# Layer 2's q by seven products, with PSUM rings kept by hand, in a four-layer attention network on one core

## The chip, the core and the metric

The kernel runs on one core of a Trainium2 chip. All data are f32. The metric is the device time in microseconds (us) of one execution. The program is given as a median of several executions; a profile comes from one further execution, which has its own time and, inside it, a span from the first to the last record.

## What is computed

The reference takes x of 4 images with C = 512 channels and 32x32 = 1024 tokens, and sends it through four residual layers, each on a normalised input (groups of 16 channels in layers 0 to 3, `_gn`):

```python
# layer 0: attention with mixed heads, 8 heads of 64
q, k, v = w_q @ x, w_k @ x, w_v @ x
attn = softmax(w_head . (q^T k * hd**-0.5))           # heads mixed ahead of the softmax
attn = instance_norm(attn) * gamma + beta             # over each head's 1024x1024
x = x + (attn @ v) @ w_proj.T + b_proj
# layer 1: a gate for each channel from the channel means, through a 9-qubit circuit
x = x + gn(x) * sigmoid(circuit(mean(gn(x))) @ fc_w.T + fc_b)
# layer 2: plain attention, 8 heads
q, k, v = Wq @ gn(x) + bq, Wk @ gn(x) + bk, Wv @ gn(x) + bv
x = x + Wp @ (softmax(q^T k / 8) applied to v) + bp
# layer 3: each token attends to its 8 best of 2048 memory rows
x = x + softmax(top8(x_t @ mem.T)) @ mem
```

## The kernel before

**Stages.** `first()` loads image 0 and normalises it block by block (128 channels a block, KC = 4) while q is multiplied. The layer-0 stage then goes through the images one after another: for each, 32 steps of 32 query rows (`step`), a software pipeline in which the scores of step s, the head mixing of step s-2 and the product with v of step s-7 stand together. After the 32 steps, seven more (`STEPS` to `STEPS + LAG`) empty the pipeline; there the next image's q products are made, a block a step. Then come its k products. The output projection of an image is spread over the steps of the next; the last image's follows at the end of the stage (`put_out`). Layer 1 is a scaling that is folded into the coefficients with which layer 2's input is normalised.

**Layer 2** is a loop over the images, with 16 units each: a unit is the scores of four key blocks against 512 queries of two heads (`scores2`), their exp on ScalarE, and the product with v of the unit before (`apply2`). `pair_sum` and `sums2` gather the sums of exp on GpSimd and VectorE, `over_keys` turns them, `invert2` sums them over the partitions on TensorE, inverts them and sends them through DRAM to be broadcast (`rb`), and `finish2` multiplies the output in PSUM by them. The end of one image and the beginning of the next is called a border here: the next image's q, k and v are multiplied, and then the output projection of this one (`seven_out`), with the first scores of the next ahead of it. Layer 3 follows.

**Seven products.** At the borders k, v and the output projection are made by `seven` (L1031): a 512x512 by 512x1024 product is cut into 2x2 quarters and made of seven products of quarters, four 128x512 matmuls of two records each, thus 28 in place of 32. They need sums of quarters of the input (`input_sums`: five VectorE operations, 128x1024 each) and of the weights (`weight_sums`: five of 128x512), and sums of the products, added from PSUM by VectorE. The weights' sums overwrite two quarters of the weights in place and fill three further places (`places7`); they are made once, for image 1, and stored to DRAM for the later images (`w_sums`). q is made of eight quarter products, by `project` (L192) through `take_q2` (L1140), and evacuated by VectorE, which adds the bias and scales it by 1/8.

**PSUM.** There are eight banks of 128x512. In the layer-0 stage they are three pairs (`pairs`), `pv_bank` and `pt_bank`, chosen by index. At the change to layer 2 the pool is closed, and two new pools are opened, of three pairs (`ps_s`) and two banks (`ps_m`); these hand out buffers in the order of allocation. Small products (`small_ps`: group means and row sums) take a pair there.

**Order.** Much of the order is written out by hand: `pin` keeps instructions in program order on their engine, which holds for the products, the copies out of PSUM and most VectorE operations. What isn't pinned is placed by a scheduler. DMAs are issued by SyncE (SP), ScalarE and GpSimd, each a queue of its own.

**Lines that the steps touch.** L312/L313 statistics, L145 group means and L326 normalising in the start; L332 q of image 0; L292 ScalarE's copy of q (`put_q`); L532 product with v of layer 0, and L590 to L592 `take_out`, the copy of the finished tile out of `pv_bank`; L684 the output's last addition at the stage's end; L1183 scores of layer 2; L1177 its exp; L1056 products by channels in `seven`; L1073 ScalarE's bias copy in `seven_k`; L1220 the product with v of layer 2; L1251 the row sums.

In the tail of layer 0, `step` has `piece` (the q product and its copy L292) between the last product with v and `take_out`:

```python
        if not tiled or s >= STEPS:
            piece(b, s)
        if mixing:
            ...
        if tiled and part == 3:
            take_out(b, j)
```

Of the kernel before, what the change touches and what calls it, by code (L numbers as in the profile page):

```python
# [16 lines left out]
P = 128  # L17
B = 4
C = 512
# [22 lines left out]
def fast_net(ctx: ExitStack, tc: tile.TileContext, a: dict, out: bass.AP, flag: bass.AP):  # L42
# [21 lines left out]
    def chan(src, name):  # L64
        t = const.tile([P, KC], F32, tag=name, name=name)
        nc.scalar.dma_start(out=t, in_=src)
        return t

    gamma = const.tile([P, NH], F32, tag="gamma", name="gamma")
    nc.scalar.dma_start(out=gamma, in_=a["in_gamma"].partition_broadcast(P))  # L70
    beta = const.tile([P, NH], F32, tag="beta", name="beta")
    nc.scalar.dma_start(out=beta, in_=a["in_beta"].partition_broadcast(P))
    bproj = chan(a["b_proj"], "bproj")
    bq2 = chan(a["bq"], "bq2")
    bk2 = chan(a["bk"], "bk2")
    bp2 = chan(a["bp"], "bp2")
    fcb = chan(a["fc_b"], "fcb")

    fcw = const.tile([NQ, C], F32, tag="fcw", name="fcw")
    nc.scalar.dma_start(out=fcw, in_=a["fc_w"])  # L80
    qpar = const.tile([P, NL * NQ], F32, tag="qpar", name="qpar")
    nc.scalar.dma_start(out=qpar, in_=a["q_params"].partition_broadcast(P))
# [3 lines left out]
    ident = const.tile([P, P], F32, tag="ident", name="ident")  # L86
    make_identity(nc, ident)
    ones = const.tile([P, P], F32, tag="ones", name="ones")
    nc.gpsimd.memset(ones, 1.0)
# [13 lines left out]
    )  # L103
    NS = 32
# [71 lines left out]
    def place(at, name):  # L176

        return pairs[at % 3] if at is not None else ps_s.tile([P, 2, NB], F32, tag="sc", name=name)
# [115 lines left out]
    def first():  # L294
# [3 lines left out]
        w = I["w_q"] = eight_k([P, KC, C], "w_q0_0", 0)  # L298
        for k in range(KC):
            nc.sync.dma_start(out=xn[:, k, :], in_=x_v[0, :, k, :])  # L300
            nc.sync.dma_start(out=w[:, k, :], in_=a["w_q"][:, k, :])
        I["w_k"] = load_w("w_k", "w_k0_0", 1)
# [5 lines left out]
        def stats(k):  # L308
            mv = small.tile([P, 2], F32, tag="mv0", name=f"mv0_{k}")
            st = small.tile([P, 2, 6], F32, tag="bnst", name=f"st_a0_{k}")  # L310
            for i in range(2):
                pin(nc.vector.bn_stats(st[:, i, :], xn[:, k, i * NB:(i + 1) * NB]))  # L312
# [3 lines left out]
        def means(k):  # L316
            next(parts[k])
            next(parts[k])
# [25 lines left out]
        for k in range(KC):  # L344
            if k + 2 < KC:
                stats(k + 2)
# [2086 lines left out]
```

## Time and profile before

| what | value |
| --- | --- |
| median of 3 executions | 2555.19 us (2554.56 to 2558.83) |
| profiled execution | 2558.39 us |
| its span | 2556.6 us |
| TensorE (PE) busy | 2503.3 us |
| VectorE (DVE) busy | 1685.8 us |
| ScalarE (ACT) busy | 985.8 us |
| GpSimd (POOL) busy | 1192.5 us |
| bytes moved | 361.39 MB, mean 141 GB/s |
| mean granted clock of TensorE | 0.998 |

The profile names groups of instructions by line, engine and operation: `pair<-xn_all,w_q` is a product into the PSUM pair from these two operands, and xN counts records. A f32 matmul of 128x128 by 128x512 is two records. "Waits" are idle times of an engine, with the engine that ended them and the line of the instruction on which it waited. The chain of waits is followed back from the last instruction of the program. Windows give busy times in a stretch of the span; PEclk is the share of full clock that TensorE was granted there.

### The profile page before, as it was taken

To read this page: it belongs to the slowest core of one execution; us is meant where nothing else is said; L and a number is where in the kernel's file an instruction comes from. 1 tells how busy PE (TensorE), PEld (TensorE's weight loads), DVE (VectorE), ACT (ScalarE), POOL (GpSimd) and SP (SyncE) were. 2 spreads that over 40 slices of the span, in tenths; PEclk is the share of its full clock that TensorE was granted. 3 is DMA by queue.
4 is the path that set the end of the run, shared out by engine and by line. 5 is a ranking of instruction groups with operands and counts; after the bars stand their busy time and mean duration, and the time that the engine had idled before them with its cause. 6 is when DMAs were issued, how large, how long until landed. Compare 5 with 4: busy or idle time off the path is not lost.

```text
span 2556.6 us, 47828 instructions
## 1 busy us (share of the span) xinstructions
PE 2503.3 (98%) x18534; PEld 1180.8 (46%) x18534; DVE 1685.8 (66%) x2785; ACT 985.8 (39%) x1177; POOL 1192.5 (47%) x1700
## 2 busy tenths in 40 slices
PE   8999999999999999999999999999999999999998
PEld 3344534554355534555633533453353344444445
DVE  4599448872688438881267567576657648788875
ACT  1467336651666336651153145125314612121211
POOL 3266415553465425553074147117405617566655
PEclk9999999999999999999999999999999999999999
DMA  2578438872698428982301130121014046767665
GB/s 83 145 207 237 125 120 226 244 211 74 172 243 235 131 82 211 244 248 101 124 16 55 70 112 18 54 83 59 21 54 148 18 130 190 219 186 217 187 184 170
DMA packets 187211, 361.39 MB, mean 141 GB/s; under 512 B 32729, under 2 KB 96217, under 8 KB 182882
## 3 DMA queue, kind: packets, MB, share of 16 engines
q1 hardware_dynamic: 105744, 178.71, 22.6%
q0 software_dynamic: 49152, 142.79, 20.6%
q10 hardware_dynamic: 32082, 36.76, 5.3%
q8 instruction: 149, 2.44, 0.4%
q14 instruction: 84, 0.69, 0.1%
HBM read 186.96 MB, written 36.96 MB: 88 GB/s over the span
## 4 chain that ended last, share of the span: by engine, by line
PE 74%; issue 10%; POOL 7%; DVE 3%; ACT 3%; DMA 2%; POOLq 0%; SPq 0%; ACTq 0%; DVEq 0%
PE pair L192 10%; PE sc_c L1183 9%; PE pv_c L1220 9%; PE pv L532 8%; POOL got L1360 7%; PE pair L467 6%; PE pair L493 5%; PE pt L425 5%; PE pt L721 4%; PE q L192 3%; PE Wk L1056 3%; PE Wv L1063 3%; ACT e L500 2%; PE Wp L1056 2%; PE at L1335 2%
## 5 line engine op out<-in xcount | busy, mean ns | idle before, releaser
L482 POOL DMA_DIRECT2D s<-ss x512 | 258.2, 511 | 399.5 <-PE pair L493 113.4
L506 DVE STREAM_TRANSPOSE eT<-e 128x1024 f32<-128x1024 f32 x256 | 316.5, 1236 | 193.6 <-ACT e L500 193.0
L1360 POOL DMA_INDIRECT got<-in_mem,ix x256 | 279.5, 1092 | 213.2 <-issue 122.1
L1177 ACT ACTIVATE eT<-sc_c 128x1024 f32<-128x1024 f32 x256 | 248.0, 1022 | 330.7 <-PE sc_c L1183 204.8
L521 DVE BATCH_NORM_STATS2 st<-e 128x6 f32<-128x256 f32 x1024 | 350.7, 404 | 0.0
L500 ACT ACTIVATE e<-pair 128x1024 f32<-128x1024 f32 x256 | 250.7, 1022 | 167.5 <-PE pair L493 137.2
L1201 POOL TENSOR_TENSOR e<-eT 128x1024 f32<-128x1024 f32 x96 | 232.3, 2421 | 168.6 <-DVE out L1125 69.5
L467 PE MATMUL pair<-k,q 64*32 64x512 f32 x4096 | 267.4, 598 | 12.7 <-ACT e L500 12.7
L473 ACT COPY ss<-pair 128x1024 f32<-128x1024 f32 x256 | 247.3, 1020 | 77.5 <-DMA s<-ss 37.9
L532 PE MATMUL pv<-eT,v 128*64 128x128 f32 x4096 | 250.7, 276 | 8.9 <-ACT pv L592 8.9
L532 PEld LDWEIGHTS pv<-eT,v 128*64 128x64 f32 x4096 | 221.1, 137 | 76.7 <-issue 54.5
L1183 PE MATMUL sc_c<-q,k 64*128 64x512 f32 x1024 | 240.9, 607 | 3.1 <-DVE xr L684 2.3
L1220 PE MATMUL pv_c<-eT,v 128*64 128x512 f32 x1024 | 233.0, 597 | 0.0
L1202 DVE TENSOR_TENSOR eT<-eT,e 128x1024 f32<-128x1024 f32 x96 | 136.3, 1420 | 146.3 <-POOL e L1201 146.1
L1197 POOL TENSOR_TENSOR eT<-eT 128x1024 f32<-128x1024 f32 x32 | 77.8, 2433 | 206.8 <-ACT eT L1177 202.8
L1407 DVE SCALAR_TENSOR_TENSOR acc<-got,et,acc 128x512 f32<-128x512 f32 x210 | 157.9, 752 | 7.5
L493 PE MATMUL pair<-s,wmix 32*32 32x512 f32 x4096 | 160.6, 600 | 2.3 <-issue 2.1
L1183 PEld LDWEIGHTS sc_c<-q,k 64*128 64x128 f32 x1024 | 93.6, 187 | 141.0 <-issue 71.9
L1340 ACT COPY att<-at 128x1024 f32<-128x1024 f32 (+1 forms) x65 | 64.9, 999 | 219.7 <-PE at L1335 212.9
L467 PEld LDWEIGHTS pair<-k,q 64*32 64x32 f32 x4096 | 57.0, 105 | 179.9 <-ACT e L500 86.2
L1220 PEld LDWEIGHTS pv_c<-eT,v 128*64 128x64 f32 x1024 | 68.0, 137 | 136.8 <-issue 136.8
L1335 PE MATMUL at<-memT,xn_d 128*128 128x512 f32 x256 | 120.7, 594 | 0.0
(335 smaller groups left out, 3431.3 us busy)
## 6 DMA issues: line engine op xcount, KB each, us to landing
s<-ss SPq DMA_DIRECT2D x512, 128.0 KB
s<-ss POOLq DMA_DIRECT2D x512, 128.0 KB
rb<-r POOLq DMA_DIRECT2D x64, 128.0 KB
o<-o SPq DMA_DIRECT2D x32, 256.0 KB
xr<-in_x ACTq DMA_DIRECT2D x32, 256.0 KB
x<-xr SPq DMA_DIRECT2D x32, 256.0 KB
xr_c<-x SPq DMA_DIRECT2D x32, 256.0 KB
rb_c<-r SPq DMA_DIRECT2D x64, 128.0 KB
```

The source lines that it names most:

```text
L192: pin(nc.tensor.matmul(ps[:, n, :], w[:, k, m * P:(m + 1) * P], rhs(k, n), start=(k == 0), stop=(k == KC - 1),))
L467: pin(nc.tensor.matmul(sc[m * NS:(m + 1) * NS, r, :], q[r * HD:(r + 1) * HD, m, s * NS:(s + 1) * NS], k_[r * HD:(r + 1) * HD, m, n * NB:(n ...
L482: pin(relays[side].dma_start(out=s2[2 * m + r::NH], in_=ss[m * NS:(m + 1) * NS, r, :]))
L493: pin(nc.tensor.matmul(mixed(s, r // 2)[t * NS:(t + 1) * NS, r % 2, :].rearrange("p (qq k) -> p qq k", qq=2), wmix[r * NS:(r + 1) * NS], s ...
L500: pin(nc.scalar.activation(e[:, half].rearrange("p r qq k -> p (r qq k)"), flat2(mixed(s, half)), AF.Exp))
L506: pin(nc.vector.transpose(eT[:, j % 2].rearrange("p b (qq i r) x -> p i r qq b x", qq=2, i=4)[:, i, 2 * half:2 * half + 2], e[:, half].rea ...
L521: pin(nc.vector.bn_stats(st[:, i, 2 * half + r, qq, :], e[:, half, r, qq, :]))
L532: pin(nc.tensor.matmul(pv[r * HD:(r + 1) * HD, gp, :], I["v"][:, t, g * HD:(g + 1) * HD], eT[:, j % 2, t, :, 4 * g:4 * g + 4], start=(t == ...
L1177: pin(nc.scalar.activation(e, scs[len(es)], AF.Exp))
L1183: pin(nc.tensor.matmul(sc[:, r, :], I["k"][r * HD:(r + 1) * HD, m, t * P:(t + 1) * P], I["q"][r * HD:(r + 1) * HD, m, n * NB:(n + 1) * NB] ...
L1220: pin(nc.tensor.matmul(pv[r * HD:(r + 1) * HD, :], I["v"][:, t, h * HD:(h + 1) * HD], e[:, r, :], start=(t == 0), stop=(t == TC - 1),))
L1360: pin(nc.gpsimd.indirect_dma_start(out=got[:, i, :], out_offset=None, in_=a["mem"], in_offset=bass.IndirectOffsetOnAxis(ap=ix[:, i:i + 1], ...
```

## The change

There are five parts.

1. **Start.** The small constants' loads on ScalarE's queue are held and issued after SP's first loads in program order; the first block of x is loaded in halves, and its statistics are taken by halves; the identity is built after the group-mean matrix. The group coefficients of `first()` are worked out by VectorE from PSUM, where GpSimd had three steps. Seventeen 128x128 products of `ones` with itself, whose result isn't used, are put among the first instructions of TensorE (`warm`).
2. **Tail of layer 0.** From step 32 on `take_out` stands ahead of `piece`.
3. **PSUM.** The pool of the layer-0 stage stays open. Layers 2 and 3 take pairs from a ring (`next_pair`) and banks in turn (`next_bank`). With `late`, from the third score block of the second unit of images 1 to 3, two places of the ring are exchanged. Between `at_border[0] = True` and `False` small products take the bank that isn't in use. k, v and the output projection at the end of layer 0 get other pairs (`m + 1 + last`, `i + 1`, `m + 2`).
4. **q of images 1 to 3 in layer 2** is made by seven products (`seven_by_channels`, which k uses too), with ScalarE's bias copies and VectorE's additions. The sums of Wq are made for image 1 in the unit loop of image 0 from s = 9 on, one operation a unit; the sums of Wq and Wp go to DRAM with their three further places (`w_more`) and share these places. The factor 1/8 is taken in exp.
5. **Order at the borders.** The input sums begin in the unit loop; the last `apply2` comes ahead of q; `over_keys` of the last unit follows it; `invert2`, `finish2` and the weight sums have other places among the products.

The diff, cut to what the steps speak of:

```diff
+    later = []
+    def held(shape, name, src):
+        t = const.tile(shape, F32, tag=name, name=name)
+        later.append(lambda: nc.scalar.dma_start(out=t, in_=src))
...
+        for n in range(2):
+            nc.sync.dma_start(out=xn[:, 0, n * NB:(n + 1) * NB], in_=x_v[0, :, 0, n * NB:(n + 1) * NB])
         for k in range(KC):
-            nc.sync.dma_start(out=xn[:, k, :], in_=x_v[0, :, k, :])
+            if k > 0:
+                nc.sync.dma_start(out=xn[:, k, :], in_=x_v[0, :, k, :])
             nc.sync.dma_start(out=w[:, k, :], in_=a["w_q"][:, k, :])
+        for load in later:
+            load()
...
-            next(parts[k])
-            next(parts[k])
+            mv = parts[k][0]
+            ps = small_ps(f"gps_a0_{k}")
+            pin(nc.tensor.matmul(ps[:, 0:1], gavg, mv[:, 0:1], start=True, stop=True))
+            dm, sq, gm = (column(name, k) for name in ("dm", "gsq", "gm"))
+            pin(nc.vector.tensor_sub(dm, mv[:, 0:1], ps[:, 0:1]))
+            pin(nc.vector.scalar_tensor_tensor(sq, dm, dm, mv[:, 1:2], ALU.mult, ALU.add))
+            pin(nc.vector.tensor_copy(gm, ps[:, 0:1]))
+            found[k] = gm, dm, sq
         def deviations(k):
-            next(parts[k])
-            found[k] = next(parts[k])
+            gm, dm, sq = found[k]
+            ps = small_ps(f"gps2_a0_{k}")
+            pin(nc.tensor.matmul(ps[:, 0:1], gavg, sq, start=True, stop=True))
+            ve, rstd = column("gve", k), column("grstd", k)
+            pin(nc.vector.tensor_scalar_add(ve, ps[:, 0:1], GN_EPS))
+            pin(rsqrt(rstd, ve))
+            found[k] = gm, rstd, dm
+        def warm(times):
+            for _ in range(times):
+                pin(nc.tensor.matmul(pairs[2][:, 0, 0:P], ones, ones, start=True, stop=True))
...
+        warm(11)
+        for i in range(2):
+            stats(0, i)
         means(0)
-        stats(1)
+        stats(1, 0)
+        warm(2)
         deviations(0)
+        stats(1, 1)
+        warm(2)
+        normalize(0)
         means(1)
-        normalize(0)
+        warm(2)
         for k in range(KC):
             if k + 2 < KC:
-                stats(k + 2)
+                for i in range(2):
+                    stats(k + 2, i)
...
+        if not plain and key in w_more:
+            for i in range(3):
+                nc.sync.dma_start(out=places7[key][i], in_=w_more[key][:, i])
...
-        add7(s1, a11, a22)
-        sub7(s7, a12, a22)
-        add7(a12, a11, a12)
-        sub7(s6, a21, a11)
-        add7(a21, a21, a22)
+        for fn, out, x, y in (
+                (add7, s1, a11, a22), (sub7, s7, a12, a22), (add7, a12, a11, a12),
+                (sub7, s6, a21, a11), (add7, a21, a21, a22)):
+            fn(out, x, y)
+            yield
         nc.sync.dma_start(out=w_sums[key], in_=w)
+        if key in w_more:
+            for i in range(3):
+                nc.sync.dma_start(out=w_more[key][:, i], in_=places7[key][i])
...
-            ps = ps_s.tile([P, 2, NB], F32, tag="sc", name=f"{key}_{b}_{at}")
+            ps = next_pair()
...
-    def seven_k(b):
-        dst = img[b]["k"] = big("k", f"k2_{b}")
+    def seven_by_channels(b, name, bias):
+        dst = img[b][name] = big(name, f"{name}2_{b}")
         def begin(i, j, ps):
             for m in range(2 * i, 2 * i + 2):
                 pin(nc.scalar.activation(
                     dst[:, m, j * NB:(j + 1) * NB], ps[:, m % 2, :],
-                    AF.Identity, bias=bk2[:, m:m + 1]))
-        return seven(b, "Wk", img[b]["xn"], by_channels, lambda ps: ps,
+                    AF.Identity, bias=bias[:, m:m + 1]))
+        return seven(b, "W" + name, img[b]["xn"], by_channels, lambda ps: ps,
...
-            I["q"][:, m, :], ps, bq2[:, m:m + 1], SCALE, ALU.add, ALU.mult)), f"q2_{b}")
+            I["q"][:, m, :], ps, bq2[:, m:m + 1], None, ALU.add)), f"q2_{b}")
...
-            pin(nc.scalar.activation(e, scs[len(es)], AF.Exp))
+            pin(nc.scalar.activation(e, scs[len(es)], AF.Exp, scale=SCALE))
...
-            sc = ps_s.tile([P, 2, NB], F32, tag="sc", name=f"sc_{nm}_{t}")
+            sc = next_pair(i >= 2 and b > 0 and u == UNITS2[1])
...
-        if t0 == TC - 4:
+        if t0 == TC - 4 and ends:
...
-            I["pv", m, n] = ps_m.tile([P, NB], F32, tag="mm", name=f"pv_c{b}_{m}_{n}")
+            I["pv", m, n] = next_bank()
...
-        ps = ps_s.tile([P, 2, NB], F32, tag="sc", name=f"rs_{nm}")[:, 0, 0:NS]
+        ps = small_ps(f"rs_{nm}")[:, 0:NS]
...
+        if s >= STEPS and tiled and part == 3:
+            take_out(b, j)
         if not tiled or s >= STEPS:
             piece(b, s)
         if mixing:
...
             exps(old, 0)
             exps(old, 1)
             turn_keys(old, 0)
-        if tiled and part == 3:
+        if tiled and part == 3 and s < STEPS:
...
-            ks[m](m + 1)
+            ks[m](m + 1 + last)
...
-                take_v2(0, i, i + 2)
+                take_v2(0, i, i + 1)
             for m in range(KC):
-                put_out(b, m, m)
-    stage.close()
-    pairs.clear()
+                put_out(b, m, m + 2)
     by_scalar.append(True)
-    stage = ctx.enter_context(ExitStack())
-    ps_s = stage.enter_context(tc.tile_pool(name="ps_s2", bufs=3, space=PSUM))
-    ps_m = stage.enter_context(tc.tile_pool(name="ps_m2", bufs=2, space=PSUM))
+    turns = [0, 0]
+    ring = [0, 1, 2]
+    def next_pair(late=False):
+        if late:
+            ring[0:2] = ring[1::-1]
+        ring.append(ring.pop(0))
+        return pairs[ring[-1]]
+    def next_bank():
+        turns[1] += 1
+        return (pv_bank, pt_bank)[turns[1] % 2]
+    at_border = [False]
     def small_ps(name):
-        return ps_s.tile([P, 2 * NB], F32, tag="sc", name=name)
+        return (pv_bank, pt_bank)[(turns[1] + 1) % 2] if at_border[0] else flat2(next_pair())
...
+    places7["Wq"] = places7["Wp"]
...
             if s == 5 and last:
                 img[b]["Wp"] = load_w("Wp", f"Wp2_{b}")
             if s >= 1:
-                scores2(b, u, UNITS2[s - 1])
+                scores2(b, u, UNITS2[s - 1], last or u != UNITS2[-1])
             for _ in range(2):
                 if s >= 3 and last:
                     next(behind, None)
-                if s >= 8:
+                if s >= 7:
                     next(ahead, None)
+            if s == 9 and b == 0:
+                weights = weight_sums(1, "Wq")
+            if s >= 10 and b == 0:
+                next(weights, None)
+            if s == len(UNITS2) - 2 and not last:
+                run_out(ahead)
+                first7, rest7 = input_sums(img[b + 1]["xn"])
+                first7[0]()
         run_out(ahead)
+        if not last:
+            first7[1]()
+            first7[2]()
+        apply2(b, UNITS2[-1])
         if last:
-            apply2(b, UNITS2[-1])
             atts[0] = attention(*tiles[0], lambda: invert2(b))
             finish2(b)
             put_out2(b)
             continue
-        early, later = input_sums(img[b + 1]["xn"])
-        for m in range(KC):
-            take_q2(b + 1, m)
-            if m < 3:
-                early[m]()
-            if b == 0 and m < 2:
-                weight_sums(1, ("Wk", "Wv")[m])
+        over_keys(b, *UNITS2[-1][:2])
+        at_border[0] = True
+        for i, _ in enumerate(seven_by_channels(b + 1, "q", bq2)):
+            if 1 <= i < 3:
+                rest7[i - 1]()
+            if i == 4:
+                invert2(b)
+            if i == 5 and b == 0:
+                run_out(weight_sums(1, "Wk"))
             next(behind, None)
         load_sums(b, "Wp", b == 0)
-        apply2(b, UNITS2[-1])
-        for i, _ in enumerate(seven_k(b + 1)):
-            if i == 0:
-                invert2(b)
-                for fn in later:
-                    fn()
-            if i == 4 and b == 0:
-                weight_sums(0, "Wp")
+        for i, _ in enumerate(seven_by_channels(b + 1, "k", bk2)):
+            if i == 1:
+                finish2(b)
+            if b == 0 and i == 2:
+                run_out(weight_sums(1, "Wv"))
+            if b == 0 and i == 4:
+                run_out(weight_sums(0, "Wp"))
             next(behind, None)
-        finish2(b)
-        early, later = input_sums(img[b]["o"])
+        first7, rest7 = input_sums(img[b]["o"])
         for i, _ in enumerate(seven_v(b + 1)):
             if 2 <= i < 5:
-                early[i - 2]()
+                first7[i - 2]()
             elif i >= 5:
-                later[i - 5]()
+                rest7[i - 5]()
             next(behind, None)
         run_out(behind)
+        at_border[0] = False
         scores2(b + 1, UNITS2[0])
         seven_out(b)
```

## The prediction

> **What bounds the kernel now.** I read the busy line first, then TensorE's waits by the engine that ended them, then the chain of waits, and last the timeline around each wait.
>
> ```profile
> span 2556.6 us, 47828 instructions
> PE 2503.3 (98%) x18534; PEld 1180.8 (46%) x18534; DVE 1685.8 (66%) x2785; ACT 985.8 (39%) x1177; POOL 1192.5 (47%) x1700
> ```
>
> TensorE is busy for 98% of the span, so a change pays only by giving it fewer matmuls, by shortening its waits, or by sparing it half clock. The waits (total, count, longest) that the change touches:
>
> ```profile
> PE pv L532 <- ACT pv L592: 8.9, 15, 1.6
> PE pt L145 <- DVE mv L313: 7.3, 1, 7.3
> PE sc_c L1183 <- DVE xr L684: 2.3, 1, 2.3
> PE Wk L1056 <- ACT k L1073: 2.0, 1, 2.0
> ```
>
> The chain (start, us, engine, target, line, records) gives the borders of layer 2: q is 64 records in 27.66 us, one 128x512 matmul being two, so 32 matmuls at 0.864 us; k at the second border, 28 matmuls with no wait, takes 3.63 + 20.80 = 24.4 us. At the first border the same k stops for 2 us before 1419.80.
>
> ```profile
> 1267.48 8.83 PE sc_c L1183 x32
> 1382.40 27.66 PE q L192 x64
> 1413.65 3.65 PE Wk L1056 x8
> 1419.80 7.13 PE Wk L1056 x16
> 1637.85 3.63 PE Wk L1056 x8
> 1641.72 20.80 PE Wk L1056 x48
> ```
>
> The timeline of a tail of layer 0 (start, busy us, what, idle and its releaser in brackets) shows ScalarE waiting out a 7 us product before it copies the output tile:
>
> ```profile
> 287.83 7.13 PE L192 MATMUL pair<-xn_all,w_q 128*128 128x512 f32 x16
> 296.55 1.97 PE L532 MATMUL pv<-eT,v 128*64 128x128 f32 x32 [1.59 <-ACT pv L592]
> 295.00 1.01 ACT L292 COPY q<-pair 128x1024 f32<-128x1024 f32 x1 [6.86 <-PE pair L192]
> 295.91 0.59 ACT L592 COPY pv<-pv 128x512 f32<-128x512 f32 x1
> ```
>
> **What the Trainium skill says.** "TensorE: Matmul & The Clock Gate", Part 1 (What's actually happening): the array runs at half clock until it has been busy for a window of about 3.4 us, and an idle window throttles it again. The trace agrees: the clock is half until 15.03 us, and again for 3.41 us after the 2.3 us wait at 1267. The same page (Back-to-back issue gap) has about 216 ns for a 512-wide pass; an f32 record here takes 432, two passes. "VectorE: DVE Perf Modes", the TRN2 errata section, gives (N+151)/0.96 ns for an f32 add, 691 ns at 512; the trace has 690, and 1220 at 1024. "DMA: Bandwidth & Descriptors" (Queues, rings and completion order) says that a queue's descriptors are consumed in ring order; that is what the last rival rests on.
>
> **The change part by part.** Sums are against the profiled execution, 2558.39 us (span 2556.6), and carried over to the median, 2555.19, which lies 3.2 below it.
>
> *q by seven products.* At three borders 32 matmuls become 28: 4 x 0.864 = 3.46, x3 = **−10.4**; I take −10.3. Beside it VectorE loses four q copies (1.28 each) and gains eight adds from PSUM (about 1.2 each), 5 us more in 24. It was busy 20.6 of 27.6 there at the first border, with three input sums (1.22) and ten weight-sum adds (0.69); of these the input sums move ahead of q and half of the weight sums to k. So it stays under 24, and k (12.1 of 24.6 at the second border) has room. ScalarE gets 4 x 2 bias copies of 0.69, and it was idle. Three pairs of PSUM give a pair two products (6.9 us) to be emptied, and the longest queue I find ahead of a release is five weight-sum adds and the release's own, 5 x 0.69 + 1.2 = 4.7 us. Nothing; without that cover, the 1 to 2 us a border of the second rival.
>
> *Wq's sums* (first image only): five adds of 0.69 (128x512), one in each of five units of the b=0 loop, and four stores on SP's queue (1.8 MB), which stand among the row sums' small ones. VectorE is busy there 33 of 43 us, and the row sums come ready 1.4 to 5 us before TensorE needs them, so each add costs 0 to 0.5: +0.3, range 0 to +2.5. One more unit takes its share of normalising (from s=7), which is neutral.
>
> *SCALE into exp*: the same ScalarE instruction with a scale. 0, at most a few ns x 256.
>
> *Tile copied out ahead of q.* Waits at 296.55, 583.23 and 873.64: 1.59 + 1.47 + 1.47 = 4.53. With the copy ahead of put_q, and pv ready before q begins, the 0.59 us copy lies beside the 7 us product. put_q then comes no later, as ScalarE is free. The fourth tail has q emptied by VectorE and no such wait. I leave 0.2 for residues: **−4.3**, range −3.5 to −4.5. The other twelve waits on that copy, 0.3 each, stay.
>
> *Rings by hand at the stage change.* The pools of layer 2 opened only when every PSUM tile was drained, so the first scores waited 2.32 us for VectorE's last output add, then met half clock. Two windows (us, busy of PE, PEld, DVE, ACT, POOL, then granted clock, DMA share, GB/s):
>
> ```profile
> 1267.70:1271.10 3.40, 3.40 (x10) 1.60 (x10) 0.81 (x4) 1.02 (x1) 0.00 (x0) 0.50 0.60 172
> 1271.20:1275.00 3.80, 3.80 (x20) 1.76 (x18) 0.00 (x0) 3.80 (x5) 2.78 (x2) 1.00 0.14 50
> ```
>
> The same number of records takes twice as long. These 32 records took 8.83 against 7.27 for a usual unit: 1.5 lost. After the change the outputs lie in pairs 2, 0, 1, 2 and the scores take 0, 1, 2: the first two pairs have been emptied for long, only the third can wait, about 0.4 us. With no idle window of that size I expect no throttling. 2.3 + 1.5 − 0.4 = **−3.4**, range −2.3 (clock lost all the same) to −4.0.
>
> *Row sums out of the ring at borders.* At the first border rs and the group means took two of three pairs, and k waited 1.96 for ScalarE to empty one. In the other two borders that wait isn't there (1637.85 + 3.63 to 1641.72 is 0.24). A free bank takes the small sums now: **−1.9**. The swap that leaves out seven_out's last pair for the next scores acts only from u=UNITS2[1], i≥2 with b>0; the scores right after seven_out take 4.62 instead of 3.66 as before. 0 to −2 over three borders; I take 0.
>
> *Start.* TensorE waits 7.28 us for the first statistics, and multiplies at half clock until 15.03:
>
> ```profile
> 11.31 3.78 PE L332 MATMUL pair<-xn_all,w_q 128*128 128x512 f32 x4 [0.97 <-DVE xn_all L326]
> 13.78 1.29 DVE L312 BATCH_NORM_STATS2 st_a<-xn_all 128x6 f32<-128x512 f32 x2 [2.53 <-DMA xn_all<-in_x]
> 15.10 1.96 PE L332 MATMUL pair<-xn_all,w_q 128*128 128x512 f32 x4
> ```
>
> Seventeen dummy products keep the clock up: 4 matmuls took 3.78 instead of 1.96 once it was full, so up to 1.8 there, and the shorter statistics chain (no POOL steps) perhaps 1 more, and the split first load 0.5. But VectorE's third set of statistics waits for xn2's landing at 13.76 and stands ahead of the normalising of the second block, so the second block's products can't begin much before 17 unless xn2 comes earlier. It may: the small loads on ScalarE's queue no longer go first. Or later, where SP's loads still wait for earlier ones to land (w1's issue at 8.32 did). Bounds: −4 (clock, chain and load all gained) and +1 (first products earlier, same landing, dummies in the way). I take **−1.5**. The circuit's evacuation of k afterwards has some 5 us of slack, so a gain isn't swallowed there.
>
> *Order at the borders.* The last apply goes ahead of q, over_keys after it: the same instructions. finish2 now heads VectorE's k adds at the second product. At borders 2 and 3, SP's queue has Wp (1.05 MB) and two of its three sum blocks (0.26 MB each) ahead of the last row sums' broadcast. At the 300 GB/s of such a load before (0.9 MB in 3 us) that is 5 us after q's end at 24.2; r to finish2 took 4.9 us before: about 34.5 us into q. TensorE needs it by 24.2 + 4 x 3.46 − 1.9 = 36.2, when k's fifth product wants the second's pair. 0, with 2 us to spare; if the load took twice as long, +3 x 2.
>
> Sum: −10.3 − 4.3 − 3.4 − 1.9 − 1.5 + 0.3 = **−21.1**. Profiled about 2537.3, median **2534**.
>
> **Rivals.**
> - *The start gives nothing and the added VectorE work shows*: landings set the start, the units of the b=0 loop lose 0.3 each. 2534 + 1.5 + 1.5 to 2534 + 2.5 + 4: 2537 to 2541. For it: the xn2 wait of 2.53 above. Against: the loads' order changes too. Chance 0.17.
> - *Waits move instead of going*: the third pair keeps the drain and the half clock (+2.5), q's adds lag and stall the ring by 1 to 2 us a border (+3 to +6): 2539.5 to 2544. For it: the first border is the one with VectorE fullest. Against: k by the same scheme has no wait at the other two. Chance 0.11.
> - *The start gains all its parts*, and the swap one or two more: 2528.5 to 2531. Chance 0.09.
> - *Slower*: finish2, held by the loads ahead of its broadcast, stops VectorE, so the ring of three and TensorE, at two borders. It eats the whole gain (21) and 5 more only when finish2 comes 13 us after 36.2, a load of 1.57 MB taking 20 us, under 80 GB/s; at 60 GB/s it is 26 us, 19.5 late each: 2534 + 39 = 2573. For it: nothing else protects the order of that queue. Against: 3 us for 0.9 MB before. Chance 0.04.
> - The change not doing what it says: q's matmul count is in the code, so only the waits could. Part of the second.
>
> **How the numbers follow.** Forecast 2531 to 2537: 0.59. The range takes in the third rival's 2529 and the second's lower part to 2543, leaving out about 0.1. A measurement can tell 0.2%, 5.1 us. Only a loss of 16 of the 21 would give no change: 0.03, slower 0.04, faster 0.93.
>
> **What would show it.** In the profile after: L192's q gone from the borders, 56 records of about 24.2 us in its place; no wait of pv on L592 over 0.5; no half clock at the stage change; no 2 us wait of Wk on ScalarE; PE's first 30 us shorter by 1 to 2. It would be wrong if a wait of Wq or Wk products on VectorE's adds or on finish2's broadcast appeared, over 1 us at each border, or if the first products waited longer for xn2.

## The result and the profile after

The changed kernel takes 2544.22 us (2536.31 to 2550.28, 8 executions), against 2557.22 for the kernel before in the same comparison: a ratio of 0.9951, interval 0.9936 to 0.9966, or 12.5 us. It was forecast at 2534, a gain of 21. It is faster, but by little more than half of the forecast (the interval allows 9 to 16 us), and its executions spread over 14 us where those of the kernel before spread over 5 (over 7 to 12 in the comparisons further down). The profiled execution took 2542.66 us. Its busy line:

```profile
span 2540.9 us, 47898 instructions
PE 2497.0 (98%) x18544; PEld 1181.0 (46%) x18544; DVE 1718.5 (68%) x2810; ACT 1000.7 (39%) x1201; POOL 1201.3 (47%) x1688
```

TensorE is busy for 6.3 us less. TensorE's waits in the changed kernel (total, count, longest):

```profile
PE pt L142 <- DVE eT L1314: 4.9, 2, 2.5
PE pv L561 <- ACT pv L621: 4.3, 12, 1.0
PE pair L1288 <- DVE s_c L1274: 2.0, 1, 2.0
PE pt L326 <- DVE mv L318: 1.7, 1, 1.7
PE pt L1257 <- DVE eT L1314: 1.0, 1, 1.0
```

Read against the list of before: pv's wait on its copy is down from 8.9 to 4.3, and the waits of 2.3 (stage change) and 2.0 (k) are gone. In their place stands a wait that the list of before doesn't have: 4.9 us of the group means (L142) on `finish2` (L1314).

From the start of named matmuls in both traces I made a table of stretches, in us. The row "first products end" has the start of the last of their records. "Border" is from the last scores of an image to the first scores of the next; "tails" are the three ends of layer 0's images; "stage" is from layer 0's last scores to the second unit of layer 2; "loop" is the rest of image 0's units. The last two columns are kernels from the experiments below, `means` and `q8`.

```
                    before     changed    later means   q by eight
first products end   27.83      28.16       28.26         30.08
tails                80.61      78.95       78.95         78.95
                     84.29      82.63       82.62         82.63
                     84.17      82.63       82.67         82.78
stage               143.86     139.78      139.79        140.92
loop, image 0       105.43     106.65      106.65        105.42
border 1             89.39      85.10       84.94         91.44
border 2             84.75      85.37       81.39         84.41
border 3             84.76      83.67       81.39         84.84
```

The tails and the stage change did what was forecast. The start did not, the loop lost 1.2, and the second and third borders gave 0.6 of loss and 1.1 of gain where 3.5 each was forecast. Outside the table, image 1's units take 2.4 us longer, which is the wait of 2.0 us on L1288 and what follows it; the other stretches of layer 0 moved by −3.2 in sum and the last part of layer 3 by −1.8, up to its last matmul. Layer 0's are chance: a second profile of the same changed kernel is 4.2 us later by the end of layer 0.

The timeline of TensorE in the changed kernel, second border (start, busy us, what, idle and its releaser):

```profile
1597.11 3.70 PE L1093 MATMUL pair<-sums,eT 128*128 128x512 f32 x8
1603.27 0.59 PE L142 MATMUL pt<-mv_d,gavg 128*128 128x4 f32 x2 [2.46 <-DVE eT L1314]
1603.72 8.57 PE L1093 MATMUL pair<-sums,Wq 128*128 128x512 f32 x16
1612.27 7.11 PE L1093 MATMUL pair<-xn_c,Wq 128*128 128x512 f32 x16
```

One product into q, the group means of the image before (`norm3`) want their bank, `pt`, and wait 2.46 us for `finish2` to read it. The next 16 records take 8.57 us where the same number takes 7.11 right after: half clock, as two windows show (us, busy of PE, PEld, DVE, ACT, POOL, granted clock, DMA share, GB/s):

```profile
1603.28:1606.68 3.40, 3.40 (x6) 1.85 (x7) 2.31 (x4) 0.16 (x1) 0.60 (x3) 0.50 0.18 53
1606.70:1610.10 3.40, 3.40 (x9) 1.49 (x9) 1.13 (x1) 0.00 (x0) 0.00 (x0) 1.00 0.52 178
```

TensorE's row sums and VectorE's timeline in the same place show what `finish2` waited for:

```profile
1589.97 0.31 PE L1288 MATMUL pair<-s_c,same 128*64 128x32 f32 x4
...
1593.78 3.37 DVE L1239 TENSOR_TENSOR eT<-eT,e 128x1024 f32<-128x1024 f32 x1 [2.27 <-POOL e L1238]
1597.07 0.34 DVE L1293 RECIPROCAL ri_c<-ri_c 128x32 f32<-128x32 f32 x1
...
1602.52 0.69 DVE L1314 TENSOR_TENSOR eT<-pt,rb_c 128x512 f32<-128x512 f32 x1 [1.16 <-DMA rb_c<-r]
```

The row sums were multiplied at 1589.97. Their reciprocal stands in VectorE's order behind an addition that waits 2.27 for GpSimd and then takes 3.37; it comes at 1597.07, and the way through DRAM takes until 1602.5. The same place in the kernel before:

```profile
1602.38 0.31 PE L1251 MATMUL rs<-s_c,same 128*64 128x32 f32 x4
1613.06 0.28 PE L145 MATMUL gps_d<-mv_d,gavg 128*128 128x4 f32 x2
...
1605.31 1.23 DVE L1202 TENSOR_TENSOR eT<-eT,e 128x1024 f32<-128x1024 f32 x1 [2.54 <-POOL e L1201]
1606.46 0.35 DVE L1256 RECIPROCAL ri_c<-ri_c 128x32 f32<-128x32 f32 x1
...
1612.57 0.68 DVE L1277 TENSOR_TENSOR eT<-pv_c,rb_c 128x512 f32<-128x512 f32 x1
```

There the chain from row sums to `finish2` took 10.2 us, against 12.5 here, because the addition took 1.23; and the group means took a pair, and came after 7 us of q. So two things meet. The group means ask earlier, and `finish2` comes 2.3 us later after its row sums. By an estimate from these numbers, a chain of 10.2 us would have freed the bank at about 1600.9, and the group means asked at 1600.8. No run shortened the chain, and why the addition is stretched was not tested.

### The profile page after: what moved, and what is told of

Read it like the earlier page. It is cut to its first block, busy times and chain, and to the rows that moved or that the text cites. A ratio compares the mean times of both kernels' runs of the same rounds, so it can differ in the third digit from the quotient of the medians.

```text
span 2540.9 us, 47898 instructions
## 1 busy us (share of the span) xinstructions
PE 2497.0 (98%) x18544; PEld 1181.0 (46%) x18544; DVE 1718.5 (68%) x2810; ACT 1000.7 (39%) x1201; POOL 1201.3 (47%) x1688
## 4 chain that ended last, share of the span: by engine, by line
PE 71%; issue 10%; POOL 9%; DVE 4%; DMA 3%; ACT 2%; SPq 0%; POOLq 0%; ACTq 0%; DVEq 0%
PE pair L189 12%; PE pv L561 8%; PE pair L1220 8%; POOL got L1397 7%; PE pair L1093 7%; PE pair L496 6%; PE pair L522 5%; PE pt L454 5%; PE pt L1257 4%; PE pt L750 4%; PE pv L1257 3%; PE pair L1100 3%; ACT e L529 2%; DMA s<-ss 2%; PE pair L1372 2%
## 5 line engine op out<-in xcount | busy, mean ns | idle before, releaser
L1214 ACT ACTIVATE eT<-pair 128x1024 f32<-128x1024 f32 x256 | 248.0, 1022 | 342.4 <-PE pair L1220 221.0
L1238 POOL TENSOR_TENSOR e<-eT 128x1024 f32<-128x1024 f32 x96 | 238.3, 2486 | 167.8 <-ACT eT L1214 122.3
L1220 PE MATMUL pair<-q,k 64*128 64x512 f32 x1024 | 239.5, 604 | 1.4 <-DVE out L1027 0.3
L1239 DVE TENSOR_TENSOR eT<-eT,e 128x1024 f32<-128x1024 f32 x96 | 148.3, 1545 | 128.8 <-POOL e L1238 128.6
L1220 PEld LDWEIGHTS pair<-q,k 64*128 64x128 f32 x1024 | 92.3, 186 | 139.2 <-issue 67.0
L1377 ACT COPY att<-pair 128x1024 f32<-128x1024 f32 (+1 forms) x65 | 64.9, 999 | 219.6 <-PE pair L1372 183.5
L1372 PE MATMUL pair<-memT,xn_d 128*128 128x512 f32 x256 | 120.7, 594 | 0.0
L1372 PE MATMUL pair<-memT,eT 128*128 128x512 f32 x256 | 120.4, 593 | 0.0
L1372 PE MATMUL pair<-eT,xn_d 128*128 128x512 f32 x256 | 120.3, 592 | 0.0
```

The costliest lines, as they stand in the source:

```text
L1214: pin(nc.scalar.activation(e, scs[len(es)], AF.Exp, scale=SCALE))
L1220: pin(nc.tensor.matmul(sc[:, r, :], I["k"][r * HD:(r + 1) * HD, m, t * P:(t + 1) * P], I["q"][r * HD:(r + 1) * HD, m, n * NB:(n + 1) * NB] ...
L1372: pin(nc.tensor.matmul(sc[:, i0 - lo:i0 - lo + NB], xn3[b][:, k, tt * P:(tt + 1) * P], memT[k][:, i0:i0 + NB], start=(k == 0), stop=(k == ...
```

## The experiments

All ratios are to the kernel before on the same chip.

**same: the changed kernel again.** No edit.

> The changed kernel once more, nothing edited, to have it on the same chip as the three that follow and to have a second profile. My theory (small sums at the second and third border go into a bank that the last output still holds, so TensorE waits for finish2; row sums late behind loads of the W blocks) expects both waits of the group means on finish2 again, 2.0 to 2.8 us each, and a wait of the row sums of 1 to 2.5 us in the second unit of image 1. The rival (the shortfall is chance: DMA noise of one execution) expects those waits at other places or gone. Ratio to before 0.994 to 0.996.

0.9964 (0.9952 to 0.9977). Both waits on `finish2` are there, 2.58 and 2.38 us: they are no chance. The 2.0 us wait of the row sums in image 1 is absent, so that one comes and goes, and that part of the expectation failed. The ratio lies a little above the expected 0.994 to 0.996.

**means: the group means after q's third product instead of its first.**

```diff
-            next(behind, None)
+            if b == 0 or i >= 2:
+                next(behind, None)
```

> The group means of the image before are asked for three products later in q at the second and third border; nothing else. If the bank is the cause, the two waits on finish2 (2.46 and 2.43 us) vanish with the 3.4 us of half clock that followed one of them, and the time falls by 4.5 to 7 us against the changed kernel on the same chip. If the q scheme itself is the cause (VectorE too late with its additions), another wait of the same size takes their place and the time stays within 1 us.

0.9923 (0.9910 to 0.9936), 2536.76 us. TensorE's timeline at the second border:

```profile
1597.51 3.70 PE L1093 MATMUL pair<-sums,eT 128*128 128x512 f32 x8
1601.05 7.03 PE L1093 MATMUL pair<-sums,Wq 128*128 128x512 f32 x16
1607.91 0.28 PE L142 MATMUL pt<-mv_d,gavg 128*128 128x4 f32 x2
```

The same 16 records at full clock, 7.03, and no wait; `finish2` still comes at 1603.08, so what took the wait away is the later place of the asker. What is left is a wait of 0.38 at each border. Both borders are at 81.39, 3.4 below the kernel before. Against the mean of changed and same (0.9958) this is 0.0035, some 9 us; the intervals allow about 4 either way. The borders of the traces give 4 and 2.3 us against the changed kernel, 2.4 and 2.2 against same: with 4.6 to 6.3 in all they fit the expected 4.5 to 7, and they don't account for the rest of the 9. Unlike the waits, the half clock isn't there each time: in six profiles of kernels with these two waits it followed 5 of 12, at 1.5 us and more. The longest is in the kernel "start" below:

```profile
1825.45 0.59 PE L145 MATMUL pt<-mv_d,gavg 128*128 128x4 f32 x2 [2.41 <-DVE eT L1285]
1825.89 10.18 PE L1064 MATMUL pair<-sums,Wq 128*128 128x512 f32 x16
```

10.18 instead of 7.03: 3.1 us lost behind a wait of 2.4. This can explain a part of the wide spread of the changed kernel. The five executions of `means` lie within 3 us; but those of the later kernels without the waits (order1, warm1, best, loop8, final) spread over 3 to 7.

**dma: loads of weights held behind the output projection.** The loads of the sums of Wq, Wk and Wv and the projection's row loads and stores are pinned in program order on SP.

> The loads of Wq's, Wk's and Wv's sums for images 2 and 3 are held in program order behind the row loads and stores of the output projection. If these loads (3.1 MB and 0.8 MB more than before) make the output projection's rows late, VectorE's wait for a row (0.74 and stretched operations) and the 2.0 us wait of the row sums in image 1's second unit go, and the time falls by 1 to 2.5 us. If VectorE's own work is the cause, the wait stays at 1.5 to 2.5 us.

0.9952 (0.9937 to 0.9967), no clear difference from the changed kernel. The 2.0 us wait is absent, but it was absent in same as well: nothing can be concluded. It came back in one later kernel (loop8, 1.99), so two of these profiles have it. Its cause stays open; in the changed kernel's chain a row load of the projection took 8.74 us and ended 18 us ahead of it.

**early: Wq's sums in units 4 to 8.**

```diff
-            if s == 9 and b == 0:
+            if s == 3 and b == 0:
                 weights = weight_sums(1, "Wq")
-            if s >= 10 and b == 0:
+            if s >= 4 and b == 0:
                 next(weights, None)
```

(with `load2` at s == 2 for image 0)

> The five additions for Wq's sums, and the weights' loads, stand six units earlier in image 0's loop, where VectorE has no normalising to do. If they are what made finish2 late there, the wait of 1.04 us at the fourteenth unit and the 0.7 us wait on the input sums at the border go: 1 to 2 us less than the changed kernel. If the earlier start of the normalising (from s=7) or the input sum in the loop is the cause, at least one of the two waits stays.

0.9951 (0.9935 to 0.9966): no difference from the changed kernel that the time can tell. In the trace the waits fall from 1.04 to 0.53 and from 0.70 to 0.25: smaller, and not gone.

**tile: the kernel before with the tile copied out first.**

> The kernel before with one edit: in the tail of layer 0 the tile is copied out ahead of the q product. The prediction's step expects the three waits of pv on that copy (1.59, 1.47, 1.47 us) gone and 4.3 us less (0.9983 of before). The rival, that q's copy is late by the 0.6 us and its reader waits, expects a new wait of scores or of the next q product of about 0.6 us at each tail, so 2.5 to 3 us less.

0.9980 (0.9972 to 0.9989), 5.1 us by the ratio. TensorE's wait is

```profile
PE pv L532 <- ACT pv L592: 4.3, 12, 1.0
```

with 12 in place of 15, and no new wait in the tails: they are 1.65, 0.75 and 1.54 shorter. (In the second, the wait of 1.47 is gone too, but records of the head mixing at 550 us, ahead of q, came 0.8 us later.) The step stands.

**rings: the kernel before with the ring by hand, no exchange of places.**

> The kernel before with the PSUM pool of layer 0 kept open through layers 2 and 3 and its pairs and banks handed round by hand; small products stay in the pairs' ring, q is made by eight. The prediction's step expects the first scores of layer 2 to wait 0.3 to 0.4 us instead of 2.32 and no half clock after it: 3.4 us less (0.9987). The 1.96 us wait of k at the first border has to stay, as rs and the group means still take two pairs; were it gone, the ring and not the small sums made it.

1.0047 (1.0033 to 1.0061): slower, which I hadn't expected at all. The stage did what was expected, 143.86 to 140.35 us, and k's wait stayed, as expected. But:

```profile
PE pair L1183 <- DVE out L993: 9.9, 3, 3.3
...
PE pair L1056 <- ACT k L1073: 2.0, 1, 2.0
```

The first line is new: right after the output projection, the third score block of the second unit now gets the pair of the projection's last product, which VectorE hasn't emptied. It is 3.3 us for each of three images, with half clock behind it in images 1 and 3: from the second to the fourth unit 20.1, 18.4 and 20.0 us, where the kernel before needs 15.4. The same block waits for nothing that long in the kernel before. I infer that its pools didn't hand out buffers in plain turn, as I had taken for granted; the traces don't name the buffers, so this is argued and not shown.

The wait of 2.0 us of k is followed by half clock here, and in tile as well: border 1 is at 91.09 in both, against 89.39 in the profile of before. Taking that wait away is therefore worth up to 3.7 us, where the prediction had 1.9.

**noswap: the changed kernel without the exchange of places.**

```diff
-            sc = next_pair(i >= 2 and b > 0 and u == UNITS2[1])
+            sc = next_pair()
```

> The changed kernel without the exchange of two places of the ring ahead of the third score block of the second unit of images 1 to 3. The prediction gave the exchange nothing. In the kernel of before with the rings by hand and no exchange, three waits of 3.3 us stood there, two of them with half clock (10.9 us together beyond the usual loss). If the exchange prevents these in the changed kernel too, this is 8 to 13 us slower than the changed kernel. If the ring's phase differs here, so that another pair comes up, it is within 1 us.

1.0026 (1.0019 to 1.0033): 2561.89 us, worse than the kernel before. TensorE in images 1 and 2:

```profile
1491.61 3.79 PE L1220 MATMUL pair<-q,k 64*128 64x512 f32 x8 [6.20 <-DVE out L1027]
...
1716.49 2.51 PE L1220 MATMUL pair<-q,k 64*128 64x512 f32 x8 [3.30 <-DVE out L1027]
```

Waits of 6.2, 3.3 and 3.3, half clock after each; the second to fourth units take 8.0, 4.6 and 5.7 us longer than with the exchange. That is more than expected. Without the exchange the whole gain of the change is gone.

**start: the changed kernel with the start of before.** Loads, statistics and means as before, no dummy products.

> The changed kernel with the start of the kernel before (loads, statistics, no dummy products). The prediction gave the start 1.5 us: then this is 1.5 us slower than the changed kernel, the last of the first products ending at 29.5 or later. The rival (landing of the third block and the granted clock set the start) expects that end within 0.5 us of 27.8 to 28.2 and no change in time that can be told.

0.9948 (0.9934 to 0.9962), the end of the first products at 28.48. In four profiles with the old start that end is at 27.83 to 28.59, mean 28.21; in eight with the new it is at 26.93 to 30.08, mean 28.09. No gain of the start shows.

**q8: the changed kernel with q by eight.** Its matmuls are those of the kernel before; the sums of Wq, their stores and loads are left out.

> The changed kernel with layer 2's q by eight products at the borders, Wq's sums, their stores and loads left out; order, rings and the rest as changed. Seven products saved 10.3 us by the prediction's count. If that saving is real and the bank's waits are tied to the short first product, q8 gives 10.3 back, but its first product lasts 7 us, so the group means find the bank free (two waits of 2.4 us gone) and the two waits in image 0's loop (1.0 and 0.7) go as well: 3 to 6 us slower than the changed kernel. If the seven products gain nothing (VectorE's additions in the way), q8 is as fast or faster.

0.9968 (0.9956 to 0.9980). The group means find their bank, since the first product lasts 7 us: no wait on `finish2` in the list, and the loop of image 0 is at 105.42, as before. Borders 2 and 3 take 84.41 and 84.84, against 81.39 with seven products and late means: 3.0 and 3.4 us, the counted 3.46. At border 1 q8 has a wait of 1.86 of its own (k on a sum of weights) and half clock after it. Seven products save what was counted, when nothing waits behind them. In time q8 is 2.6 us above the mean of changed and same, where 3 to 6 were expected; the intervals allow about 4 either way.

**order1: normalising ahead of the next block's statistics** in the start, on top of means.

> The later group means, and in the start VectorE normalises a block ahead of the statistics of the block after it, instead of behind them. Two theories of why the start gained nothing: the landing of the third block ahead in VectorE's order, or the half clock into which the dummy products' pauses let TensorE fall (full from about 5 to 9 us, half to 15.6). If the landing alone limits, the end of the first products comes 1 us or more earlier, at 27.2 or before (28.26 in the kernel with the later means alone). If the clock limits as well, the first eight products still end at about 17.3 and the end stays within 0.5 us of 28.2.

0.9946 (0.9932 to 0.9959). Both theories failed: the end came later, at 29.91.

```profile
PE pt L326 <- DVE mv L318: 4.2, 3, 1.5
```

Moved back, the statistics are late for the means, for which TensorE now waits three times, 4.2 us in all, where it waits twice and 2.7 in `means`. The order of the change is the better one of the two.

**warm1: eight dummy products in place of two** ahead of the second means, on top of means.

> The later group means, and eight dummy products in place of two ahead of the second block's means, to fill the pause of 1.7 to 2.4 us in which the clock is lost. If the clock alone limits, the first eight products end by 15.2 instead of 17.3 and the end comes at 26.5. If the landing limits as well, the second block still waits until 16.8, a new wait of TensorE on VectorE's normalising appears there, and the end is at 27.6 to 27.9.

0.9926 (0.9912 to 0.9939), like means alone in time; the end is at 27.00. Two windows of the changed kernel, and the same two of this one:

```profile
9.25:12.65 3.40, 2.97 (x8) 2.12 (x9) 1.46 (x6) 0.00 (x0) 0.39 (x2) 0.50 0.83 286
12.65:16.05 3.40, 3.40 (x7) 1.67 (x6) 1.56 (x5) 0.00 (x0) 0.55 (x2) 0.50 1.03 390
```

```profile
9.25:12.65 3.40, 3.22 (x15) 2.00 (x15) 1.18 (x5) 0.00 (x0) 0.19 (x1) 1.00 0.88 280
12.65:16.05 3.40, 1.79 (x6) 0.64 (x4) 2.25 (x5) 0.00 (x0) 0.74 (x2) 1.00 1.05 431
```

The change's dummies got the clock up by 5.8 us, but left a pause of 1.74 ahead of the second means, and the first real products ran at half clock from 9.2 to 16.1. Filled, the pause costs no clock; the first eight records of q end early, and then TensorE waits for VectorE:

```profile
16.19 1.99 PE L354 MATMUL pair<-xn_all,w_q 128*128 128x512 f32 x4 [1.10 <-DVE xn_all L348]
```

The first eight records ("products" in the expectations) end 3.3 us earlier (14.06 against 17.37), and this wait and the one before it leave 1.2 of that. It is between the two expectations, nearer to "both limit". The 1.2 is not shown to be a gain: the end of kernels with the start as in the change swings over 3 us from profile to profile, and dma, with two dummies in that place, ended at 26.93. In q8, also with two, the clock stayed full until 17.8, the first eight records ended at 13.94, and yet the end was the latest of all, 30.08, behind waits of 2.14 and 1.10.

**best: means, early, order1 and warm1 together.**

> Later means, Wq's sums early in image 0's loop, VectorE's new order in the start and the eight dummy products together. If landing and clock both limit the start, the end of the first products is at 26.4 to 27.0; with the waits of 1.0 and 0.7 us in image 0's loop halved the time is 1.5 to 3 us below the kernel with the later means alone (0.9923 of before): 0.9913 to 0.9918. If the two parts of the start don't add up, 0.992.

0.9929 (0.9916 to 0.9943), the end at 28.31, where 26.4 to 27.0 was expected: with order1's place of the statistics TensorE waits for the means three times again (2.8 us in all), and the wait in image 0's loop is 1.36 us. A miss.

**loop8: means and early, and the normalising of the next image from the ninth unit on, as before.**

```diff
-                if s >= 7:
+                if s >= 8:
                     next(ahead, None)
```

> Later means, Wq's sums early, and the next image's normalising back at the ninth unit (s from 8) as in the kernel before. Open is which of the two moves makes finish2 late in image 0's loop (1.04 us with the sums from the tenth unit on, 0.53 us with the sums early, 1.36 us with the sums early in another run). If the earlier normalising is the cause, the wait is below 0.2 us here. If Wq's sums are, wherever they stand, 0.5 us or more stays. If it is chance of DMA, it can be anything from 0 to 1.4.

0.9909 (0.9895 to 0.9923), 2534.45 us: faster than the kernel before and the changed one, and the lowest ratio of all, though its interval overlaps those of `means` and warm1. By the ratio it is 23 us below the kernel before (20 to 27), so with these edits the forecast gain of 21 is there. The loop is at 105.42 with no wait on `finish2`. As q8 has the normalising from the eighth unit and no Wq sums, and is at 105.42 too, neither alone shows a cost in these profiles; the two together do. Wq's sums in their place of the change, with the normalising from the ninth unit, were not run.

**final: means, early and warm1**, with the normalising as in the change.

> Later means, Wq's sums early, eight dummy products in place of two; VectorE's order in the start as in the changed kernel. From the parts: start 1.2 us below the kernel with the later means alone, image 0's loop and its border 0.5 to 1 us below: 0.9915 to 0.9920 of before. If the parts are within chance, 0.9920 to 0.9930.

0.9927 (0.9912 to 0.9942). The loop is at 107.53, worse than in early (106.14), and the parts don't add up: with the sums and the normalising both in it, the loop's end swings from 0.7 to 2.1 above 105.4, and there `finish2` also waits for its own DMA.

## Why the prediction was wrong, step by step

The gain is 8.6 us short of the forecast 21.1. By the traces, most of that is two waits for a PSUM bank that the prediction held to be free: 4.9 us, and about 1.6 of half clock behind them. The rest is the start and the loop of image 0.

- *q by seven products, −10.3*: the mechanism and the size hold, 3.0 and 3.4 at borders 2 and 3 between `means` and q8; border 1 can't be compared, as q8 has a wait of its own there. No lag of VectorE on q's additions was seen.
- *Tile copied out, −4.3*: right, 4.9 in the trace of the change, and in tile 3.9 in its trace and 5.1 (2.8 to 7.2) by its ratio.
- *Stage change, −3.4*: right, −4.1 in the trace and −3.5 in rings. The third pair waits 0.31, as said.
- *Row sums out of the ring, −1.9*: **here it failed.** "A free bank takes the small sums now" was read from the code's name for it. At the first border that is so (1.96 gone, 0.29 in its place). At the other two the first small sum is the group mean, one product of q after the last apply, and the bank still holds the output that `finish2` has to read. That is 4.8 to 5.4 us in the six profiles of kernels with this order and q by seven, and in 5 of 12 cases half clock on top. The step "the last apply goes ahead of q ... the same instructions" is the other half of it: before, the asker came 7 us of q later and took a pair. I priced the removal of a resource's old user and never asked who holds the new one. Nor did I price that `finish2` would come 2.3 us later after its row sums, by which the wait is as long as it is. My own sign of being wrong, a wait on `finish2` of over 1 us at a border, came, but in front of this small product and not of q's or k's. It is the second rival's kind of outcome, waits that move instead of going, with another cause than I gave it (VectorE's lag in q, the stage's drain). That its upper end, 2544, was measured is luck: its terms, 2.5 and 3 to 6 on top of 2534, reach only 2542.5.
- *The exchange of places, 0*: against the kernel before it is 0, as said, but not because it does nothing. Without it the changed kernel loses 8.0 + 4.6 + 5.7 us.
- *Start, −1.5*: about 0. The first eight records run at half clock in most profiles, since the dummies leave a pause; and where they don't (warm1, final, q8), TensorE waits for VectorE at the second block, so at most 1.2 is left of it. The first rival's reason, the landing ahead of VectorE's statistics, fits this but was not tested apart.
- *Image 0's loop, +0.3*: +1.2 in the trace; the 0.7 at the first products of the border, counted below with the 0.29, may belong to it as well. The term was Wq's adds alone; in the profiles the loss comes only with the earlier normalising beside them, which I had called neutral.
- *finish2 behind Wp's load* (the slower rival): not seen. At the second border the last `finish2` came without a wait of its own at 1627.90, and k's first addition waited for TensorE. (The working there, 24.2 + 5 + 4.9, gives 34.1 and not 34.5.)

Summed with what the traces show: −10.3 − 4.9 − 4.1 − 1.9 + 1.0 (waits in the first border) + 1.2 + 4.9 + about 1.6 (half clock, at 5 of 12 and 1.5 to 3.1 each) = −12.5, and 12.5 was measured. That the two agree to the tenth is luck: the terms come from single profiles, the measured gain can be 9 to 16, and left out are the 2.4 us in image 1, the half clock at the end of layer 0 (below) and that behind k's wait in the kernel before, each there in some profiles only. Not settled: what makes the row sums of image 1 late in some executions, and how much of the spread is that.

## What to carry to other kernels

When a small product is taken off a full ring into a "free" bank, look up who wrote that bank last and when its reader comes, in the order after the change and not before it: here a product of 0.4 us, issued in the order of the program, held TensorE for 2.4 us, and in 5 of 12 cases the half clock cost 1.5 to 3.1 us more. A ring kept by hand replaces a choice that the pools made; follow each buffer past the slowest evacuation before calling the change neutral. Dummy products kept the clock for the first real ones only where no long pause was left between them (warm1); and even then the work after them has to be ready, or the time goes into a wait.

## What the runs showed of the hardware

- In six profiles, waits of 2.4 to 3.0 us brought a half clock of 3.4 us (once 6.8) in 5 of 12 cases, at 1.5 to 3.1 us of loss. "TensorE: Matmul & The Clock Gate" (Part 1, What's actually happening) calls the window free-running, which fits the same wait being followed by half clock in one profile and not in another. The page also has an idle window of about 3.4 us ahead of half clock. Here shorter waits were enough, the 2.32 of the kernel before among them, which the prediction took for agreement.
- In the traces the clock changes after whole multiples of 3.413 us (in the kernel before from 15.03 to 1267.72, 367 of them). Cut into such windows, the 12 waits sort themselves: where half clock followed, TensorE was busy for 0.8 to 1.5 us of the window that held most of the wait; where it didn't, for 1.6 to 2.2 us. In the kernel "start" a wait of 2.39 kept the clock and one of 2.41 lost it; the windows of the two waits, and the one after each:

```profile
1603.39:1606.81 3.42, 1.66 (x4) 0.38 (x2) 2.31 (x3) 1.73 (x4) 0.00 (x0) 1.00 0.22 79
1606.81:1610.22 3.41, 2.79 (x8) 1.47 (x9) 2.94 (x5) 0.86 (x3) 0.60 (x3) 1.00 0.05 8
1821.85:1825.26 3.41, 1.18 (x3) 0.19 (x1) 2.27 (x3) 2.19 (x4) 0.00 (x0) 1.00 0.21 77
1825.27:1828.67 3.40, 3.22 (x6) 1.67 (x7) 2.49 (x5) 0.39 (x2) 0.60 (x3) 0.50 0.16 27
```

  This was found in the traces afterwards and not tested, and it doesn't sort every wait of another kind: in loop8 a window with 1.43 us of busy TensorE (1498.58 to 1502.00) kept full clock.
- Even a wait of 0.89 us with small products around it, at the end of layer 0, was followed by half clock at about 1203 to 1209 us in four of the profiles (same, early, best, final), at 1.7 us of loss each; the others with this wait kept full clock. The stretch "stage" is at 141.5 to 143.1 in these four, against 139.8 in seven others; the rest of the difference in same and best came earlier, in the head mixing. In the kernel "start" the stretch is at 141.44 with no half clock in it.
